# Layer 0's experts: which parts of a routed product are transposed on TensorE, and when its results are evicted

## The chip, the cores and the metric

The kernel runs on one core of a Trainium2 chip. The metric is device microseconds from the start to the end of one execution, lower is better. Three runs of the kernel before gave 1381.71, 1381.80 and 1383.36 us, median 1381.8. The engines are TensorE (PE, with its weight loads PEld), VectorE (DVE), ScalarE (ACT), GpSimd (POOL) and SyncE (SP, which here only issues DMAs).

## The reference

Four layers follow one another, each an attention over a context and a feed-forward block, on x of 4 batches x 256 tokens x 256 columns, in float32. The change lies in the feed-forward block of layer 0, 64 "arrows" of rank 16:

```python
def _L0_ffn_ref(x, A, B, W, bias):
    TOPK = 4
    vecs = jnp.einsum('arh,bsh->bsar', A, x)
    arrows = jnp.linalg.norm(vecs, axis=-1)
    _, idx = jax.lax.top_k(arrows, TOPK)
    routes = jax.nn.one_hot(idx, arrows.shape[-1], dtype=x.dtype).sum(-2) / TOPK
    v = jnp.einsum('bsa,bsar->bsr', routes, vecs)
    delta = jnp.einsum('bsa,ajr,bsr->bsj', routes, B, v)
    base = jnp.einsum('bsh,jh->bsj', x, W) + bias
    return base + delta
...
x = x + _L0_ffn_ref(_layernorm(x, axis=-1), L0_ffn_A, L0_ffn_B, L0_ffn_W, L0_ffn_bias)
```

For a token s, delta is a product over 64 x 16 = 1024 terms: route of arrow a times v of rank r, times B. The kernel needs these 1024 numbers u[a, r] with tokens in columns, as the stationary operand of eight matmuls of 128 rows each.

## The kernel before

All work of the four engines PE, ACT, DVE and POOL stands in an order written out by hand: inside `tc.manual_schedule` each of these engines executes its instructions in the order of the program text. SP is not among them. A DMA started through `nc.gpsimd` takes its place in POOL's order, one through `nc.scalar` in ACT's.

**Attention 0** (loops from line 1707): for each batch b and each of four groups of heads, two steps i = 2 hg + kp. A step does `scores` (PE, then ACT exponentials), `values` of the group before and, each second step, `quotient` (two stream transposes, a reciprocal and a product on DVE, additions on POOL). Between the steps `between(b, i)` (line 1613) places other work: in batches 0 to 2 the projections of the next batch, with a chain on DVE, ACT and PE (`sum`, `power`, `root`, `scaled`, `transposed`), and in batch 3 the first work of the experts. PSUM is a ring of six banks for nearly everything (tag "ring") and two banks "o".

**Experts of layer 0**: the class `Arrows` (line 1471) handles one of 8 chunks of 128 tokens (chunk n is batch n // 2, half n % 2):
- `vectors` (1479): eight matmuls of 512 columns, then squares (1493) and copies (1494) on ACT into the two halves of a tile `two`.
- `routes` (1496): on DVE the sum of squares, the four largest, the 64 routes (1509), the product of the vectors with them (1511) and v (1513); on POOL the product u of routes and v, 128 x 1024 (1514), into the second half of `two`.
- `turned` (1516): eight transposes on PE (1522) and two ACT copies (1525) into `uT`.
- `output` (1527): matmuls with ww (1531) and with wb (1535) into a bank "o", the bias added on DVE (1537), and x_sb updated on POOL (1538).

Its input rows are normalised: `Norm` (915) computes statistics on DVE and a POW on POOL (928), `tokens` (930) the normalised rows on DVE, and `layernorm_T` (939) transposes them on PE with an ACT copy. The kernel also has `layernorm_aside` (969), which does the same with two DVE stream transposes and 16 DMAs from SP, used in later layers; its scratch tile `y` has one buffer.

The loop at line 1749 runs the chunks after attention 0. Into it are mixed the **folds** of layer 1's weights (`folding`, 1003): eight steps, each with matmuls `pm` and `pn`, ACT work and a copy on DVE (1033). Each pair of steps needs one of four sets of raw weights, loaded by `load_raw` (987) in four DMAs of 512, 128, 128 and 512 KB into tiles with two buffers; the call stands in `folding` when nobody loaded the set earlier. At the end come the norm of layer 1's first rows (`a1_0`), its transposition, the squares of the context on ACT, and then layer 1's attention.

## Time and profile before

| what | value |
|---|---|
| median of 3 runs | 1381.8 us (1381.71 to 1383.36) |
| the profiled execution, its own time | 1380.97 us |
| its span, first to last instruction | 1379.2 us |
| mean granted TensorE clock | 0.999 |
| end of attention 0's last values on PE | 137.46 us |
| end of the last expert output on PE | 220.46 us |
| product u of line 1514 on POOL | 1.93 us, 8 times |
| copy of two transposes' banks, line 1525 on ACT | 0.59 us median, 16 times |
| raw weights of layer 1 on SP, first issues | 153.72 us (two sets), 181.05, 192.29 us |
| raw weights of layer 2 on POOL | 0.74 to 0.81 us for most issues |

Times in the profile are microseconds from the start of the span. A row of a timeline gives the start, the busy time, the engine, the line of the kernel, the operation, the tile written and the tiles read, the shape and how many; in brackets, how long the engine had stood idle and which instruction released it. In the chain a row gives start, length and what ran. A float32 matmul shows as two passes, a transpose as one.

### The profile page before, as it was taken

To read this page: it belongs to the slowest core of one execution; us is meant where nothing else is said; L and a number is where in the kernel's file an instruction comes from. 1 tells how busy PE (TensorE), PEld (TensorE's weight loads), DVE (VectorE), ACT (ScalarE), POOL (GpSimd) and SP (SyncE) were. 2 spreads that over 40 slices of the span, in tenths; PEclk is the share of its full clock that TensorE was granted. 3 is DMA by queue.
4 is the path that set the end of the run, shared out by engine and by line. 5 is a ranking of instruction groups with operands and counts; after the bars stand their busy time and mean duration, and the time that the engine had idled before them with its cause. 6 is when DMAs were issued, how large, how long until landed. Compare 5 with 4: busy or idle time off the path is not lost.

```text
span 1379.2 us, 20227 instructions
## 1 busy us (share of the span) xinstructions
PE 1369.2 (99%) x7221; PEld 903.1 (65%) x7221; DVE 897.2 (65%) x2052; ACT 572.6 (42%) x1134; POOL 699.4 (51%) x848
## 2 busy tenths in 40 slices
PE   9999999999999999999999999999999999999997
PEld 7665676566656667887565666666975665666666
DVE  6767863666666557655676756558656758566675
ACT  5766454433343332256434333333364334333331
POOL 5223333566565445352577655566325676444660
PEclk9999999999999999999999999999999999999999
DMA  5000220300000001361120000000432000000001
GB/s 171 15 3 2 77 78 17 89 19 8 16 5 19 0 13 43 83 218 48 47 54 15 17 0 16 0 1 16 124 119 69 7 12 4 1 8 1 0 1 34
DMA packets 77907, 50.79 MB, mean 37 GB/s; under 512 B 40628, under 2 KB 72645, under 8 KB 77799
## 3 DMA queue, kind: packets, MB, share of 16 engines
q1 hardware_dynamic: 72262, 36.13, 9.6%
q0 software_dynamic: 4176, 12.24, 3.1%
q8 instruction: 59, 0.97, 0.3%
q10 hardware_dynamic: 1360, 1.05, 0.2%
q14 instruction: 50, 0.40, 0.1%
HBM read 38.78 MB, written 6.95 MB: 33 GB/s over the span
## 4 chain that ended last, share of the span: by engine, by line
PE 97%; POOL 2%; DVE 1%; issue 0%; ACT 0%; POOLq 0%; DVEq 0%
PE ps L1948 23%; PE po L1956 23%; PE paq L1918 6%; PE pao L1918 5%; PE pbq L1918 4%; PE pbo L1918 4%; PE ps L1401 3%; PE po L1411 2%; PE pyf L1535 2%; PE paf L1485 2%; PE pgu L2496 2%; PE pm L1014 2%; PE psh L2317 2%; PE py L2042 2%; PE pn L1030 1%; PE pb L2901 1%
## 5 line engine op out<-in xcount | busy, mean ns | idle before, releaser
L1967 POOL TENSOR_TENSOR half<-pT 128x1024 f32<-128x1024 f32 x93 | 218.4, 2349 | 282.8 <-ACT pT L1951 228.0
L1948 PE MATMUL ps<-qT,cT 128*128 128x512 f32 x768 | 345.6, 593 | 0.0
L1956 PE MATMUL po<-pT,c_sb 128*128 128x512 f32 x768 | 345.3, 592 | 0.0
L1951 ACT ACTIVATE pT<-ps,mbias 128x512 f32<-128x512 f32 x384 | 263.8, 687 | 164.0 <-PE ps L1948 147.3
L1956 PEld LDWEIGHTS po<-pT,c_sb 128*128 128x128 f32 x768 | 145.8, 190 | 183.2 <-issue 183.2
L1948 PEld LDWEIGHTS ps<-qT,cT 128*128 128x128 f32 x768 | 138.9, 190 | 138.4 <-issue 136.1
L1960 ACT COPY oT<-po 128x512 f32<-128x512 f32 x96 | 56.2, 586 | 265.2 <-PE po L1956 265.2
L2003 POOL TENSOR_TENSOR oT<-oT,wide 128x512 f32<-128x512 f32 x84 | 106.8, 1291 | 0.0
L1928 DVE TENSOR_TENSOR qT<-qT,paq 128x128 f32<-128x128 f32 x90 | 25.2, 280 | 87.1 <-ACT qT L1927 87.1
L1405 ACT ACTIVATE pT<-ps 128x512 f32<-128x512 f32 x128 | 66.0, 602 | 21.6 <-PE ps L1401 21.4
L1975 DVE TENSOR_TENSOR half<-half 128x512 f32<-128x512 f32 x96 | 71.9, 749 | 2.7 <-POOL half L1965 2.5
L1977 DVE STREAM_TRANSPOSE turned<-half 128x512 f32<-128x512 f32 x96 | 68.3, 711 | 6.3
L1918 PE MATMUL paq<-xnT_a,m_sb 128*128 128x128 f32 x360 | 71.3, 280 | 0.0
L1928 DVE TENSOR_TENSOR w<-w,pao 128x128 f32<-128x128 f32 x21 | 6.0, 285 | 99.2 <-ACT w L1927 99.2
L1918 PE MATMUL paq<-xx,m_x 128*128 128x128 f32 x360 | 69.6, 275 | 0.0
L1918 PEld LDWEIGHTS paq<-xnT_a,m_sb 128*128 128x128 f32 x360 | 57.5, 192 | 18.2 <-issue 9.2
L1981 DVE TENSOR_REDUCE sums<-turned 128x16 f32<-128x512 f32 x96 | 65.9, 686 | 3.3
L1918 PE MATMUL pao<-n_x,ox 128*128 128x128 f32 x336 | 65.0, 275 | 0.0
L1927 ACT COPY qT<-paq 128x128 f32<-128x128 f32 x90 | 23.9, 265 | 94.2 <-PE paq L1918 93.2
L1931 DVE TENSOR_TENSOR qT<-qT,pbq 128x384 f32<-128x384 f32 x90 | 49.8, 554 | 9.4
L1918 PEld LDWEIGHTS paq<-xx,m_x 128*128 128x128 f32 x360 | 54.7, 192 | 0.0
L2002 DVE STREAM_TRANSPOSE wide<-rz 128x512 f32<-128x512 f32 x84 | 54.4, 686 | 0.0
(504 smaller groups left out, 2553.9 us busy)
## 6 DMA issues: line engine op xcount, KB each, us to landing
wq<-in_L_wqT SPq DMA_DIRECT2D x8, 512.0 KB
wo<-in_L_wo SPq DMA_DIRECT2D x8, 512.0 KB
yd<-yr SPq DMA_DIRECT2D x20, 128.0 KB
xnT_a<-y_a SPq DMA_DIRECT2D x144, 16.0 KB
xd<-xn_f SPq DMA_DIRECT2D x8, 256.0 KB
w<-in_F_w SPq DMA_DIRECT2D x4, 512.0 KB
wq<-in_L_wqT POOLq DMA_DIRECT2D x3, 512.0 KB
wo<-in_L_wo POOLq DMA_DIRECT2D x3, 512.0 KB
```

Of the source, the lines that this page charges most:

```text
L1405: nc.scalar.activation(pT[kp][:, j], ps[j], AF.Exp)
L1918: nc.tensor.matmul(p[:, at, :], lhsT=lhsT, rhs=rhs, start=(k == 0 and at == 0), stop=(k == len(of) - 1 and i == which[-1]),)
L1948: nc.tensor.matmul(ps, lhsT=cT[:, b, k * P : (k + 1) * P], rhs=qT, start=True, stop=True)
L1951: nc.scalar.activation(pT[:, k, :], ps, AF.Exp, bias=mbias[:, b, k : k + 1])
L1956: nc.tensor.matmul(po, lhsT=c_sb[:, b, k, :], rhs=pT[:, k], start=(k == 0), stop=(k == NK - 1))
L1960: done["head"] = nc.scalar.copy(raw, po).ins
L1967: nc.gpsimd.tensor_tensor(half, pT[:, 0:2], pT[:, 2:4], ALU.add)
L1975: nc.vector.tensor_tensor(part, half[:, 0], half[:, 1], ALU.add)
L1977: nc.vector.transpose(turned.rearrange("p f i -> p (f i)"), part)
L1981: nc.vector.tensor_reduce(sums[b, hp // 4][:, hp % 4, :], turned, AX.X, ALU.add)
L2002: nc.vector.transpose(wide, rzs[b, hp // 4][:, hp % 4, :, None].to_broadcast([P, NB, 32]))
L2003: eng.tensor_tensor(outs[b, hp], outs[b, hp], wide.rearrange("p f i -> p (f i)"), ALU.mult)
```

## The change

- `routes` no longer forms u. It leaves the routes twice side by side (128 columns) and v (16 columns). `turned` transposes only these two on PE; v's transpose goes by an ACT copy and a DMA to a DRAM tile `turned_v`, and SP reads it back so that each of 128 partitions (64 arrows, two halves) holds 8 ranks by 128 tokens in the second half of `two`. A new `spread` multiplies this in place by the transposed routes on POOL, which gives uT. wb is loaded with its rows permuted to match.
- `output` is split: the matmuls stay, the bias and the addition to x_sb become `add`, called later.
- The expert rows of batches 0 to 2 go by `layernorm_aside` (new `rows_of_arrows`), the first already in batch 2 of attention 0. Chunk 0's `vectors` move from step 4 of batch 3 to step 1, its `routes` from 5 to 2, and its `turned` and `spread` come before the end of attention 0.
- The loop over chunks is replaced by a sequence written out. Raw weights of layer 1 are loaded by POOL instead of SP, one set at a time, behind the spreads of chunks 2, 3, 4 and 6.

```diff
-            dma = (nc.gpsimd if L == 2 else nc.sync).dma_start(dst, src[a * P : (a + z) * P, :].rearrange("(h e) d -> e h d", e=P))
+            dma = (nc.gpsimd if L < 3 else nc.sync).dma_start(dst, src[a * P : (a + z) * P, :].rearrange("(h e) d -> e h d", e=P))
...
+        dram0 = ctx.enter_context(tc.tile_pool(name="f0d", bufs=1, space=bass.MemoryType.DRAM))
...
-        wb = load_fw("wb", [P, 8, D], lambda w: [(w, t["F0_bT"].rearrange("(k p) n -> p k n", p=P))], "wb", f0w)
+        wb = load_fw("wb", [P, 8, D], lambda w: [
+            (w[64 * h : 64 * h + 64], t["F0_bT"].rearrange("(a h k) n -> h a k n", h=2, k=8)[h]) for h in range(2)
+        ], "wb", f0w)
...
+        turned_v = dram0.tile([B * NC, RA, P], F32, tag="turned_v", name="turned_v")
...
-                route = small.tile([P, NA], F32, tag="route", name=f"route{u}")
-                nc.vector.tensor_scalar(route, rest[:, :NA], 0.0, 1.0 / TOPA, ALU.is_lt, ALU.mult)
-                route_b = route[:, :, None].to_broadcast([P, NA, RA])
-                nc.vector.tensor_tensor(ar, ar, route_b, ALU.mult)
-                v = small.tile([P, RA], F32, tag="v", name=f"v{u}")
-                nc.vector.tensor_reduce(v, ar.rearrange("p a r -> p r a"), AX.X, ALU.add)
-                nc.gpsimd.tensor_tensor(sq, route_b, v[:, None, :].to_broadcast([P, NA, RA]), ALU.mult)
+                self.route = sq.rearrange("p a r -> p (a r)")[:, : 2 * NA].rearrange("p (h a) -> p h a", h=2)
+                nc.vector.tensor_scalar(
+                    self.route, rest[:, None, :NA].to_broadcast([P, 2, NA]), 0.0, 1.0 / TOPA, ALU.is_lt, ALU.mult
+                )
+                nc.vector.tensor_tensor(ar, ar, self.route[:, 0, :, None].to_broadcast([P, NA, RA]), ALU.mult)
+                self.v = small.tile([P, RA], F32, tag="v", name=f"v{u}")
+                nc.vector.tensor_reduce(self.v, ar.rearrange("p a r -> p r a"), AX.X, ALU.add)
 
             def turned(self):
-                self.uT = w0.tile([P, 8, P], F32, tag="qT0", name=f"uT{self.u}")
-                for n in range(2):
-                    pt = bank("t", [P, 4, P], f"puT{self.u}_{n}")
-                    for k in range(4):
-                        a0 = 8 * (4 * n + k)
-                        nc.tensor.transpose(
-                            pt[:, k, :], self.two[:, 1, a0 : a0 + 8, :].rearrange("p a r -> p (a r)"), ident
-                        )
-                    nc.scalar.copy(self.uT[:, 4 * n : 4 * n + 4, :], pt)
+                two = self.two.rearrange("p n a r -> p n (a r)")
+                self.routeT, vT = two[:, 0, :P], two[:RA, 0, P : 2 * P]
+                self.uT = two[:, 1].rearrange("p (k s) -> p k s", s=P)
+                pt = bank("t", [P, 2, P], f"prT{self.u}")
+                nc.tensor.transpose(pt[:RA, 1, :], self.v, ident)
+                nc.tensor.transpose(pt[:, 0, :], self.route.rearrange("p h a -> p (h a)"), ident)
+                nc.scalar.copy(vT, pt[:RA, 1, :])
+                put = turned_v[self.b * NC + self.c]
+                nc.scalar.dma_start(put, vT)
+                nc.scalar.copy(self.routeT, pt[:, 0, :])
+                for h in range(2):
+                    nc.sync.dma_start(
+                        two[64 * h : 64 * h + 64, 1],
+                        put[8 * h : 8 * h + 8].rearrange("(o k) s -> o (k s)", o=1).to_broadcast([64, 8 * P]),
+                    )
+
+            def spread(self):
+                nc.gpsimd.tensor_tensor(
+                    self.uT, self.uT, self.routeT[:, None, :].to_broadcast([P, 8, P]), ALU.mult
+                )
...
+        def rows_of_arrows(k):
+            xnT = early.tile([P, ND, S], F32, tag="xf", name=f"xnT_f0_{k}", bufs=3)
+            xnTs["f", k] = layernorm_aside(norms["f"].tokens(), f"f0_{k}", xnT, True)
...
+            if b == B - 2:
+                if i == 2:
+                    norms["f"] = Norm(0, "f0_0")
+                elif i == 3:
+                    rows_of_arrows(0)
...
-                if i in (0, 2, 6):
-                    norms["f", i // 2] = Norm(min(i // 2, 2), f"f0_{min(i // 2, 2)}")
-                if i in (1, 3, 7):
-                    xns["f", i // 2] = norms["f", i // 2].tokens()
-                if i in (3, 5):
-                    k = (i - 3) // 2
-                    xnTs["f", k] = layernorm_T(xns["f", k], f"f0_{k}")
-                if i == 4:
+                if i in (0, 6):
+                    norms["f"] = Norm(1 + i // 6, f"f0_{1 + i // 6}")
+                if i in (1, 7):
+                    rows_of_arrows(1 + i // 6)
+                if i == 1:
                     arrows[0] = Arrows(0)
                     arrows[0].vectors()
+                if i == 2:
+                    arrows[0].routes()
                 if i == 5:
-                    arrows[0].routes()
+                    arrows[0].turned()
+                if i == 7:
+                    arrows[0].spread()
...
         for n in (1, 2):
             arrows[n] = Arrows(n)
             arrows[n].vectors()
-        arrows[1].routes()
-        arrows[0].turned()
+            arrows[n].routes()
         arrows[0].output()
+        arrows[1].turned()
+        arrows[0].add()
         output0(B - 1)
...
+        def vectors(n):
+            arrows[n] = Arrows(n)
+            arrows[n].vectors()
+
+        def output(n, *raw):
+            arrows[n].spread()
+            for i in raw:
+                load_raw(1, i)
+            arrows[n].output()
...
+        vectors(3)
+        norm = Norm(3, "f0_3")
+        arrows[2].turned()
+        vectors(4)
+        vectors(5)
+        arrows[3].routes()
+        arrows[4].routes()
+        output(1)
+        arrows[3].turned()
+        output(2, 0)
+        arrows[1].add()
+        xn3 = norm.tokens()
+        arrows[5].routes()
+        arrows[4].turned()
+        arrows[2].add()
+        next(fold)
+        xnTs["f", 3] = layernorm_T(xn3, "f0_3")
+        next(fold)
+        vectors(6)
+        output(3, 1)
+        arrows[5].turned()
+        arrows[6].routes()
+        arrows[3].add()
+        vectors(7)
+        context_squares(0)
+        arrows[7].routes()
+        output(4, 2)
+        arrows[6].turned()
+        context_squares(1)
+        arrows[4].add()
+        next(fold)
+        next(fold)
+        norm = Norm(0, "a1_0")
+        arrows[7].turned()
+        xn1 = norm.tokens()
+        output(5)
+        context_squares(2)
+        arrows[5].add()
+        output(6, 3)
+        context_squares(3)
+        arrows[6].add()
+        for _ in range(3):
+            next(fold)
+        first_xnT = layernorm_T(xn1, "a1_0")
+        next(fold)
+        output(7)
+        arrows[7].add()
         next(fold, None)
```

More of the change, by code (lines that the diff above doesn't have):

```diff
@@ L1535, in output, with add @@
                     nc.tensor.matmul(py, lhsT=self.uT[:, k, :], rhs=wb[:, k, :], start=False, stop=(k == 7))
+                self.py = py
+            def add(self):
+                b, c, py = self.b, self.c, self.py
                 ys = w0.tile([P, D], F32, tag="y_sb", name=f"ys{self.u}")
@@ L1747, in bounded_path @@
         fold = folding(1, *mn)
-        for n in range(B * NC):
-            if n + 2 < B * NC:
-                arrows[n + 2].routes()
-            if n:
-                arrows[n].turned()
-            if n % NC == 0:
-                if n + 3 < B * NC:
-                    arrows[n + 3] = Arrows(n + 3)
-                    arrows[n + 3].vectors()
-                for _ in range((0, 0, 1, 1, 2, 2, 1, 1)[n]):
-                    next(fold)
-                if n == 6:
-                    xn1 = norm.tokens()
-                if n:
-                    arrows[n].output()
-            else:
-                k = n // NC + 2
-                if k < B:
-                    xnTs["f", k] = layernorm_T(xns["f", k + (k == 2)], f"f0_{k}")
-                if n == 7:
-                    first_xnT = layernorm_T(xn1, "a1_0")
-                    next(fold)
-                arrows[n].output()
-                for _ in range((0, 0, 1, 1, 2, 2, 1, 0)[n]):
-                    next(fold)
-                if n + 3 < B * NC:
-                    arrows[n + 3] = Arrows(n + 3)
-                    arrows[n + 3].vectors()
-            if n == 5:
-                norm = Norm(0, "a1_0")
-            if n == 0:
-                norm = Norm(3, "f0_3")
-            if n == 1:
-                xns["f", 3] = norm.tokens()
-            if 2 <= n < 2 + B:
-                b = n - 2
-                c2 = w0.tile([P, NK, DC], F32, tag="z0", name=f"c2_{b}")
-                for k in range(NK):
-                    nc.scalar.activation(
-                        c2[:, k], c_sb[:, b, k], AF.Square, accum_out=csq[:, b * NK + k : b * NK + k + 1]
-                    )
@@ new lines, in vectors, with context_squares @@
+        def vectors(n):
[6 more added lines that the diff above has]
+            arrows[n].output()
+        def context_squares(b):
+            c2 = w0.tile([P, NK, DC], F32, tag="z0", name=f"c2_{b}")
+            for k in range(NK):
+                nc.scalar.activation(
+                    c2[:, k], c_sb[:, b, k], AF.Square, accum_out=csq[:, b * NK + k : b * NK + k + 1]
+                )
```

## The prediction

> **What bounds the kernel.** First I read the busy times and the chain that ended last:
> ```profile
> PE 1369.2 (99%) x7221; PEld 903.1 (65%) x7221; DVE 897.2 (65%) x2052; ACT 572.6 (42%) x1134; POOL 699.4 (51%) x848
> ...
> PE 97%; POOL 2%; DVE 1%; issue 0%; ACT 0%; POOLq 0%; DVEq 0%
> ```
> TensorE is the chain. Then the busy time of the stretch that changes, from the end of attention 0 to the last expert output:
> ```profile
> 137.46:220.46 83.00, 83.00 (x381) 60.79 (x382) 57.99 (x109) 41.08 (x119) 26.02 (x24) 1.00 0.21 64
> ```
> The columns are PE, PEld, DVE, ACT, POOL, clock, DMA. PE is busy in all 83.00 us: a matmul removed shortens the kernel by its own length, and a wait added to PE lengthens it by its own. Third, the chain in order of time (start, us, what):
> ```profile
> 113.97 0.16 PE pmk L1680
> ...
> 116.10 1.75 PE ps L1401 x16
> ...
> 119.88 1.07 PE ps L1401 x16
> ...
> 144.52 0.87 PE puTf L1522 x8
> ...
> 155.93 0.44 PE pxn_f L945 x4
> ```
> Fourth, DVE and POOL in order of time, whose order is that of the program:
> ```profile
> 206.18 0.69 DVE L1033 COPY n_sb<-pn 128x512 f32<-128x512 f32 x1 [1.06 <-PE pn L1030]
> 206.78 0.42 DVE L925 BATCH_NORM_STATS2 st_a<-x_sb 128x6 f32<-128x256 f32 x1
> ...
> 208.23 0.70 POOL L928 TENSOR_TENSOR rstd_a<-ve_a,neghalf 128x2 f32<-128x2 f32 x1 [2.13 <-DVE ve_a L927]
> ...
> 213.12 0.42 DVE L1537 TENSOR_TENSOR ysf<-pyf,bias 128x256 f32<-128x256 f32 x1 [2.98 <-PE pyf L1535]
> 213.62 0.73 POOL L1538 TENSOR_TENSOR x_sb<-x_sb,ysf 128x256 f32<-128x256 f32 x1 [4.69 <-DVE ysf L1537]
> ```
> Here a fold's copy, a norm and its POW on POOL, then an addition on POOL hold nobody up, since no matmul needs POOL soon after. In the new program one does.

> **Removed from TensorE.** Eight transposes of an arrow take 0.87 us (0.109 each); two remain, 0.22. Over 8 arrows: 8 x 0.65 = 5.2 us. Three `layernorm_T` for the expert rows go to DVE and DMAs: in the chain they took 0.59, 0.44, 0.44 = 1.47 us. The 1.75 us of scores after `pmk` against 1.07 elsewhere was a wait for DVE to empty the mask's bank; `vectors` of arrow 0 now stands between (3.43 us) and covers it: 0.68. **Gain: 7.35 us.** All other matmuls stay: `vectors` 3.43, `output` 0.86 + 3.45 = 4.31, a fold 0.89 + 0.86.

> **The new way of uT.** Two transposes, an ACT copy (0.25), a DMA issue on ACT (0.5 at the start of the trace), 8 KB to DRAM, two reads of 256 KB issued by SP (0.5 each), then `spread` on POOL. No row times a DMA to DRAM and back. The only load with a waiting reader is x_sb, 256 KB: issued at 0.80, first used at 3.92, so 3.1 us. Two such in sequence and the issues give about 7.1 us; below, two rows of issue alone, 1.5; above, a raw set of 1.3 MB needed 5.9 us from issue to the end of its traffic, so 12.5. I take 7.1, the nearest by size. `spread` has no row: the old product of the same size took 1.93 (two repeated operands), the addition of line 1967, also 128x1024, 2.35. With contiguous operands it is nearer to the second, and the additions of 256 and 512 columns (0.73, 1.27) extrapolate there too: 2.35, low end 1.93.

> Let T be the end of attention 0's last values (137.46 before). By the rows, PE's order after T is: vectors 1, 2; output 0; turned 1 (T+11.4); output0; vectors 3; turned 2 (16.8); vectors 4, 5; output 1 (23.7 to 28.0); turned 3; output 2 (28.2 to 32.5); turned 4; fold, transposes, fold; vectors 6 (ends 40.1); output 3. Each `output` starts with 0.86 us of ww matmuls that need no uT. Outputs 1, 2 and 3 then need `spread` finished at T+24.6, 29.1 and 41.0. Reads land at T+18.5, 23.9 and 35.3; POOL is free of the additions and the POW of batch 3's norm at T+19.6; of arrow 2's addition, behind five `routes` of 5.4 us on DVE, at T+37.5. So those spreads end at about T+22, 26.3 and 39.9: hidden, by 2.6, 2.8 and 1.1. If that cover goes, each late us is one on PE. Outputs 0 and 7 have over 4 us.

> **The waits added.** Three spreads stand on POOL behind something that only just became possible.
> Output 4: `spread` follows arrow 3's addition, which follows `routes` 6 on DVE. From the end of vectors 6: routes start after 0.67 and take 5.43 (row 185.98 to 191.43), ysf 0.42, x_sb 0.81, spread 2.40: 9.7. PE gets there after 4.31 + 0.22 + 3.43 + 0.86 = 8.8. **Wait 0.9** (0.45 with 1.93).
> Output 5: behind it on POOL is the POW of layer 1's norm; its statistics wait on DVE for the copy of the second fold just before. From the end of `pn`: copy to POW 206.14 to 208.93, 2.79, plus 2.40 = 5.2; PE has 0.22 + 0.86. **Wait 4.1** (3.7).
> Output 6: `spread` follows arrow 5's addition. From the end of output 5 the rows give 213.08 to 214.35, 1.27, plus 2.40 = 3.67, less 0.86. **Wait 2.8** (2.4).
> Sum 7.8 (6.5 to 7.8). Behind spread 5 POOL has arrow 5's addition, spread 6 and raw set 3, all of which only follow output 5 anyway; DVE's `tokens` behind the POW feed a transpose much later.

> **Smaller terms.** In batch 2, tokens (1.14 beside a POOL addition) and two stream transposes (0.83) now stand on DVE ahead of the head sums; the chain sum, power, root, pad ends at 102.85 instead of 101.9, PE wants it at 102.38, and the late exponentials hold banks: 0.5 (0 to 1.2). In batch 3, `routes` 0 on DVE delays two evictions by about 0.5 and 0.4 past the reuse of their banks: 0.6 (0 to 0.9). Raw set 0 is issued by POOL (0.75 to 0.81 a piece, 3.1 in all) only after spread 2, from T+26.3; SP's last piece landed 4.4 after its issue, so wo at T+33, just when `pn` wants it (33.6), beside the reads of arrow 3 (512 KB): 0.5 (0 to 2.5). The later sets have 5 us or more from the wait of their buffers, and SP's own queue carries 16 pieces of expert rows (0.65 each) ahead of arrow 1's reads: done at T+12.8, no later than the write. The last rows land near T+15, needed at T+16.8. The permuted wb load and 4 MB of reads ride on a DMA share of 0.21: nothing. ACT loses 1.1 us of copies an arrow and gets two short ones and an issue: nothing.

> **Sum.** 7.8 + 0.5 + 0.6 + 0.5 = 9.4 of waits against 7.35 gained: +2.05 us (-0.85 to +5.05). The profiled execution took 1380.97 (span 1379.2 and 1.8 around it), 0.8 under the median 1381.8; a difference carries over, so **1383.8**. 0.2%, 2.8 us, is about what a measurement of this kernel can tell from no change; the forecast lies within that.

> **Rivals.** (A) The forecast, 52%: the gain is real and POOL's order gives it back; own range 1380.9 to 1386.9.
> (B) Slower: the pause before output 5 lets the matrix clock fall. This trace has a slow TensorE once, after the idle start:
> ```profile
> 1.53 4.21 PE L1468 MATMUL pwarm<-ident 128*128 128x128 f32 x18 [1.53 <-POOL ident masks.py:199]
> ...
> 7.96 0.83 PE L1468 MATMUL pwarm<-ident 128*128 128x128 f32 x6
> ```
> 0.23 us a pass, later 0.11, for some 6 us, so half of 6 is lost: 3.0, giving 1386.8. It decides if 4.1 us of idle is enough; in the stretch no gap is over 0.3 us and the clock column reads 1.00, so nothing there speaks for or against. 16%.
> [...]
> (C) Slower: the DRAM round trip takes 12.5 instead of 7.1. It decides from 9.9 (29.1 - 2.4 - 16.8), where output 2's slack ends; then output 1 waits 1.7 (11.4 + 12.5 + 2.4 against 24.6), output 2, now later, 0.9, and the first fold, its weights issued behind, 2.2 in place of 0.5: +4.3, 1388.1. For it: SP and raw sets share the queues; against: the DMA share. 8%.
> (D) Faster: the three waits don't arise, because DVE or POOL comes earlier than the rows say. The gain less the smaller terms is 5.75: 1376.0. Against it: in this trace POOL and DVE keep the program's order everywhere in the stretch. That the change doesn't take work off PE can't be: the transposes are gone from its program. 24%.

> **Chances.** Of A's 52%, 0.45 lies beyond +2.8, 0.53 within and 0.02 below -2.8; B and C are slower, D faster: slower 0.47, same 0.28, faster 0.25. The range reaches down to 1375, 1 below D's value, and up to 1389, 0.9 above C's; what is left out is a bound met together with a rival.

> **What would show it.** Right: PE idle ahead of uT's matmuls three times, released by POOL's spread, near 1, 4 and 3 us; two transposes per arrow; the stretch from T to the last output near 85.5 (83.0, less 5.4 of transposes and 0.44, plus 8.3 of waits); matmuls of 0.109 a pass after the pauses. Wrong: no idle before outputs 5 and 6 (D); passes of 0.2 us behind output 5's pause (B); idle before outputs 1 to 3 released by a DMA (C); spread at another price than 1.93 to 2.35.

## The result, and the profile after

| | before | after |
|---|---|---|
| median | 1381.8 us, 7 runs, 1380.28 to 1383.45 | 1386.19 us, 7 runs, 1385.75 to 1387.07 |
| profiled execution, its span | 1380.97, 1379.2 us | 1386.06, 1384.3 us |
| mean granted TensorE clock of the profiled execution | 0.999 | 0.994 |

The changed kernel takes 1.0033 of the time before, 95% interval 1.0023 to 1.0044: some 4.4 us longer. The forecast was 1383.8 us, range 1375 to 1389.

The page of after, the busy times and the chain, against the same two lines of before:

```profile
PE 1368.5 (99%) x7161; PEld 900.0 (65%) x7161; DVE 900.4 (65%) x2058; ACT 567.1 (41%) x1131; POOL 714.0 (52%) x864
...
PE 95%; POOL 2%; DVE 1%; issue 1%; ACT 0%; POOLq 0%; DVEq 0%
```

PE has 60 rows less and is busy 0.7 us less, in a span 5.1 us longer. The stretch from the end of attention 0's last values to the last expert output (start and end, length, then PE, PEld, DVE, ACT, POOL busy, clock, DMA share, GB/s):

```profile
136.45:224.36 87.91, 80.22 (x329) 56.11 (x328) 56.42 (x103) 35.88 (x116) 40.48 (x39) 0.96 0.37 106
```

Before, PE was busy in all of its 83.00 us. Now 7.7 of 87.91 are idle, and the clock column, 1.00 before, reads 0.96. The rows of PE in order of time show both (start, busy time, what, and in brackets the idle time ahead and what ended it):

```profile
186.45 3.72 PE L1551 MATMUL pyf<-wb,twof 128*128 128x256 f32 x16 [0.86 <-POOL twof L1539]
...
199.06 6.21 PE L1551 MATMUL pyf<-wb,twof 128*128 128x256 f32 x16 [4.08 <-POOL twof L1539]
205.11 1.03 PE L1547 MATMUL pyf<-ww,xnT_f 128*128 128x256 f32 x4
208.88 3.72 PE L1551 MATMUL pyf<-wb,twof 128*128 128x256 f32 x16 [2.75 <-POOL twof L1539]
```

The brackets are the three waits for `spread`, ahead of outputs 4, 5 and 6. The second row takes 6.21 us where its neighbours take 3.72 for the same 16 passes: from 199.06 to the next row's 205.11 are 6.05 us, against 3.45 at full clock without a pause, so 2.60 lost (its neighbours, which start after a pause at full clock, lose 0.11 of that too). The clock in windows of 1 us (the last three columns are clock, DMA share, GB/s):

```profile
197.00:198.00 1.00, 0.00 (x0) 0.00 (x0) 1.00 (x1) 1.00 (x9) 1.00 (x1) 0.65 0.06 11
198.00:199.00 1.00, 0.00 (x0) 0.00 (x0) 1.00 (x1) 0.47 (x4) 1.00 (x1) 0.50 0.00 0
...
204.00:205.00 1.00, 1.00 (x6) 0.90 (x5) 0.00 (x0) 0.00 (x0) 0.00 (x0) 0.93 0.00 0
205.00:206.00 1.00, 1.00 (x6) 0.65 (x4) 0.42 (x1) 0.00 (x0) 0.19 (x1) 1.00 0.00 0
```

It falls to a half at 197.31, while PE is idle, and is back at 204.13.

A second low passage lies 375 us later, in layer 1, where the lists of tokens per expert are made. Before, and then after, PE in order of time:

```profile
565.47 4.07 PE L2429 MATMUL plist<-bring,at 128*128 128x40 f32 x32
569.37 2.84 PE L2335 MATMUL pysh<-wds,gsT 128*128 128x256 f32 x12
```

```profile
569.42 4.61 PE L2482 MATMUL plist<-bring,at 128*128 128x40 f32 x32
573.82 5.47 PE L2388 MATMUL pysh<-wds,gsT 128*128 128x256 f32 x12
```

Nothing waits here in either kernel, and the change doesn't touch these lines. Yet the twelve wide passes take 5.26 us to the next row instead of 2.68, and the whole place costs 3.3 us more, of which 0.3 comes back in the expert blocks behind it.

A third difference lies at the very start, ahead of everything that the change touches. The first matmuls run slowly in both (the first 18 passes take 4.21 us), and full speed comes sooner in the profiled execution of after. Before, and then after:

```profile
6.38 1.30 PE L1468 MATMUL pwarm<-ident 128*128 128x128 f32 x6
```

```profile
6.28 0.83 PE L1471 MATMUL pwarm<-ident 128*128 128x128 f32 x6
```

After is 0.4 us ahead from here on, by chance: in another execution of a kernel made from before, raw weights on POOL below, arrow 0's vectors start at 122.36, in before at 122.85.

So the 5.1 us of span add up from places where the same instruction can be compared in both traces: -1.0 at the end of attention 0 (first vectors at 137.39 and 136.39; -0.4 of it from the start), +4.9 in the stage (first matmul of layer 1 at 220.30 and 224.20, so +3.9), +3.0 at the lists and behind, together +6.95 at the last matmul (1371.32 and 1378.27); then -1.85, since the end of the program comes 7.2 us after the last matmul in before and 5.3 in after.

### The profile page after: what moved, and what is told of

The parts are those of the page before. It is cut to its first block, busy times and chain, and to the rows that moved or that the text cites. A ratio compares the mean times of both kernels' runs of the same rounds, so it can differ in the third digit from the quotient of the medians.

```text
span 1384.3 us, 20261 instructions
## 1 busy us (share of the span) xinstructions
PE 1368.5 (99%) x7161; PEld 900.0 (65%) x7161; DVE 900.4 (65%) x2058; ACT 567.1 (41%) x1131; POOL 714.0 (52%) x864
## 4 chain that ended last, share of the span: by engine, by line
PE 95%; POOL 2%; DVE 1%; issue 1%; ACT 0%; POOLq 0%; DVEq 0%
PE ps L2001 23%; PE po L2009 23%; PE paq L1971 6%; PE pao L1971 5%; PE pbq L1971 4%; PE pbo L1971 4%; PE ps L1404 3%; PE po L1414 2%; PE paf L1490 2%; PE pgu L2549 2%; PE psh L2370 2%; PE pyf L1551 2%; PE py L2095 2%; PE pm L1014 1%; PE pn L1030 1%; PE pb L2954 1%
## 5 line engine op out<-in xcount | busy, mean ns | idle before, releaser
L928 POOL TENSOR_TENSOR rstd_f<-ve_f,neghalf 128x2 f32<-128x2 f32 x15 | 10.6, 705 | 85.6 <-DVE ve_f L927 84.7
```

## The experiments

Each kernel was run beside the kernel before on the same chip; ratios are to before, with 95% intervals. "At the lists" is the start of the first `plist` matmul, 565.47 in before and 569.42 in after: what a trace shows there is what layer 0 gained or lost, give or take some 0.4 us by which executions of the same work differ from the start on (arrow 0's vectors start at 113.96 to 114.40 in after and the kernels made from it).

**The pause before output 5.** Layer 1's first norm is moved behind output 5.

```diff
-        norm = Norm(0, "a1_0")
         arrows[7].turned()
-        xn1 = norm.tokens()
         output(5)
+        norm = Norm(0, "a1_0")
+        xn1 = norm.tokens()
```

> Layer 1's first Norm and its tokens are put behind output(5), so output 5's spread is issued on POOL before the Norm's power and rstd work. Theory 1 (the stage lost its time to the pause of 4.08 us before output 5's wb matmuls, and to the clock of 0.50 that followed it, 2.6 us more): the pause is under 1 us and the clock stays at 1.00, so the stage is about 6 us shorter than after's 87.8; 1386.2 - 4.1 - 2.6 = 1379.5, or about 1376.5 if the second low clock (572.7 to 578.8 in after) goes too. Rival (the pause is only the place where lateness shows, and layer 1's first attention waits for its Norm instead): the pause goes, but tokens come some 4 us later and PE waits for them: 1383 to 1386.

Measured: 1379.78 us (0.9987, 0.9979 to 0.9996). The pause before output 5 is gone, and nobody waits for the norm. PE of this kernel:

```profile
195.22 3.62 PE L1551 MATMUL pyf<-wb,twof 128*128 128x256 f32 x16
...
202.45 5.41 PE L1551 MATMUL pyf<-wb,twof 128*128 128x256 f32 x16 [2.75 <-POOL twof L1539]
```

The total is as theory 1 had it, its parts aren't: the same pause of 2.75 us before output 6 that left the clock alone in after halves it here, for half as long (1.7 us lost). So the length of a pause alone does not decide.

**The pause kept, but filled.** Dummy matmuls stand between output 5's ww and wb matmuls.

```diff
-            def output(self):
+            def output(self, fill=0):
...
+                if fill:
+                    warm(fill)
...
-            arrows[n].output()
+            arrows[n].output(17 if n == 5 else 0)
```

> Seventeen transposes' worth of empty matmuls of 128x128 stand between output 5's ww and wb matmuls; all else is after's. Theory 1 (the low clock is made by PE's idle time before output 5): wb's matmuls start as late as in after, but run at 1.00, 3.4 to 3.7 us instead of 6.05; 1386.2 - 2.6 = 1383.6, or 1380.5 if the second low clock goes as well. Rival (the low clock is not tied to the idle time, but to a time in the program): wb's matmuls take 6 us all the same, and the time is 1386 or more.

Measured: 1384.75 us (1.0025, 1.0015 to 1.0036), 1.1 above the expectation. PE:

```profile
195.39 3.96 PE L1471 MATMUL pwarm<-ident 128*128 128x128 f32 x34
199.65 3.72 PE L1553 MATMUL pyf<-wb,twof 128*128 128x256 f32 x16 [0.30 <-POOL twof L1539]
203.20 1.03 PE L1547 MATMUL pyf<-ww,xnT_f 128*128 128x256 f32 x4
206.98 5.41 PE L1553 MATMUL pyf<-wb,twof 128*128 128x256 f32 x16 [2.75 <-POOL twof L1539]
```

Output 5's matmuls start as late as in after but at full clock, 3.72 us against 6.21: the low clock there comes from the idle time. What is missing to the expectation is output 6's: its pause of 2.75 us now lowers the clock, which costs 1.7 us (the lists, with one low stretch instead of two, give some of it back).

**All spreads ahead of what made them late.**

```diff
+        arrows[4].spread()
+        load_raw(1, 2)
         arrows[6].routes()
...
-        output(4, 2)
+        arrows[4].output()
...
-        norm = Norm(0, "a1_0")
         arrows[7].turned()
-        xn1 = norm.tokens()
         output(5)
+        arrows[6].spread()
+        load_raw(1, 3)
+        norm = Norm(0, "a1_0")
+        xn1 = norm.tokens()
...
-        output(6, 3)
+        arrows[6].output()
```

> All three late spreads are issued on POOL ahead of what made them late: output 4's before routes 6 and add 3, output 6's and 5's before layer 1's Norm. Theory 1 (the three waits of 0.86, 4.08 and 2.75 us and the low clock of 2.6 us are the whole loss of the change; turning only routes and vectors gains about what was forecast): 1386.2 - 7.7 - 2.6 = 1375.9, and 1372.7 if the second low clock goes too: faster than before by 6 to 9 us. Rival (the waits cover others, for the Norm's tokens or for raw weights, that end just behind them): under 4 us of it is gained, 1382 or more.

Measured: 1374.79 us (0.9949, 0.9936 to 0.9962), 7.0 us below before. At the lists it stands at 561.57, 3.9 us ahead of before and 7.85 ahead of after. Its trace has no low clock between the start and the last matmul. Two waits are left, 1.79 us before output 5 and 0.24 before output 6:

```profile
196.22 3.72 PE L1551 MATMUL pyf<-wb,twof 128*128 128x256 f32 x16 [1.79 <-POOL twof L1539]
...
201.04 3.72 PE L1551 MATMUL pyf<-wb,twof 128*128 128x256 f32 x16 [0.24 <-POOL twof L1539]
```

POOL shows a new cause:

```profile
193.82 2.35 POOL L1539 TENSOR_TENSOR twof<-twof 128x1024 f32<-128x1024 f32 x1 [0.65 <-DMA twof<-turned_v]
198.63 2.36 POOL L1539 TENSOR_TENSOR twof<-twof 128x1024 f32<-128x1024 f32 x1 [2.47 <-DMA twof<-turned_v]
```

POOL is there in time and waits for the vectors to come back from DRAM. For output 5 that took 12.2 us from the last transpose (181.59) to the spread. In after, arrow 2's trip, the only one with a wait of POOL for it, took 7.3 (153.16 to 160.48). Raw set 2 is loaded at the same time here, and the reads of `turned_v` take up to 7.2 us from issue to landing, against at most 4.0 in after.

**The spread in halves.**

```diff
-                nc.gpsimd.tensor_tensor(
-                    self.uT, self.uT, self.routeT[:, None, :].to_broadcast([P, 8, P]), ALU.mult
-                )
+                for k in (0, 4):
+                    nc.gpsimd.tensor_tensor(
+                        self.uT[:, k : k + 4], self.uT[:, k : k + 4],
+                        self.routeT[:, None, :].to_broadcast([P, 4, P]), ALU.mult,
+                    )
```

> Each spread is done as two instructions of four blocks, so that wb's first four matmuls can start after the first half. Theory 1: each of the three pauses ends about 1.2 us sooner (0, 2.9 and 1.6 us), the second half (1.2 us) ends before the first four pairs of matmuls (1.7 us) do; if the clock goes low after 4.08 us and not after 2.75, it may stay up at 2.9: 1386.2 - 3.3 - 2.6 = 1380.3, and 1382.9 if it still goes low. Rival (PE waits for the whole tile whichever half is done, or the second instruction's own start costs what the half saves): 1386, within 0.5 us.

Measured: 1382.11 us (1.0003, 0.9995 to 1.0012), runs from 1379.2 to 1383.7. The waits are 0, 3.00 and 1.68 us, each 0.9 to 1.1 shorter, so PE does start on the first half.

```profile
196.82 5.12 PE L1553 MATMUL pyf<-wb,twof 128*128 128x256 f32 x16 [3.00 <-POOL twof L1540]
```

The clock falls after 3.00 us, for one time of 3.4 us instead of two. The profiled run, the fastest of the twelve, has no low clock at the lists.

**What lowers the clock at the lists.** The next two kernels are before and after with six filling matmuls, which stand ahead of the list matmuls, split into three ahead and four in the middle.

```diff
-                for _ in range(6):
+                for _ in range(3):
                     nc.tensor.matmul(pw, lhsT=ident, rhs=ident, start=True, stop=True)
                 for n in units:
+                    if n == 8:
+                        for _ in range(4):
+                            nc.tensor.matmul(pw, lhsT=ident, rhs=ident, start=True, stop=True)
```

> The kernel before, with its six filling matmuls ahead of layer 1's list matmuls (128x40, 3.9 us without a wide one among them) split: three ahead, four in the middle (0.2 us more PE work). Theory 1 (the clock is set for one stretch of 3.41 us by how busy PE's array was in the stretch ahead of it; the list matmuls fill one such stretch in some runs and not in others, and each low stretch costs 1.7 us: that is why before's runs stand at about 1380.4, 1382.0 and 1383.6): no run has a low stretch, all lie at 1380.3 to 1381.0, clock 0.998 to 0.999. Rival (the low stretch comes from something else, power or the chip's state): the runs still spread over 1380 to 1384.

> After, with the same split of the filling matmuls; all in layer 0 stays. Theory 1: the second low clock (572.8 to 579.6, 2 stretches, 3.2 us) goes and the first (197.3 to 204.1) stays: 1386.2 - 3.2 + 0.2 = 1383.2, clock 0.997, one low passage in the trace. Rival (the second low clock follows from the first, or from anything in layer 1 but the list matmuls): 1386, two low passages.

Measured: before so mixed 1381.19 us (0.9992, 0.9983 to 1.0), after so mixed 1383.56 (1.0017, 1.0008 to 1.0025). Of the 72 runs of before beside the experiments (a 73rd, at 2841.94 us, is left out) 29 stand at 1380.2 to 1381.0, 29 at 1381.5 to 1382.5 and 14 at 1383.3 to 1384.0. Of the 11 mixed ones ten stand in one group at 1380.8 to 1381.6, up to 0.6 above the range expected, and one at 1382.8; that one was profiled, has no low clock, and lost 1.4 us in the expert blocks at 593 us, where the mix does nothing. After comes down by 2.6 us. PE of after so mixed:

```profile
569.20 2.11 PE L2485 MATMUL plist<-bring,at 128*128 128x40 f32 x16 [0.24 <-DVE at L2484]
571.14 1.14 PE L2479 MATMUL pfill<-ident 128*128 128x128 f32 x8
572.11 1.88 PE L2485 MATMUL plist<-bring,at 128*128 128x40 f32 x16
573.82 2.84 PE L2388 MATMUL pysh<-wds,gsT 128*128 128x256 f32 x12
```

The wide passes behind the lists are back at 2.84. Theory 1 holds for both: with wide matmuls among the narrow ones the twelve passes behind take 2.84 us, without them 5.47 in after, though PE is busy there all the time.

**The raw set moved out of the trip's way** (on the kernel with the spreads first).

```diff
         arrows[4].spread()
-        load_raw(1, 2)
...
-        output(5)
+        output(5, 2)
```

> The kernel with the spreads first, but raw set 2 of layer 1 is loaded behind output 5's spread instead of output 4's, so that it no longer fills the DMA queues while output 5's vectors go through DRAM. Theory 1 (that trip took 11.6 us instead of 7.2 because the raw loads moved at the same time, 1.79 us of PE's wait): the trip is 7 to 8 us, PE's wait before output 5 goes, 1374.8 - 1.8 = 1373.0. Rival (output 6's trip collides with the load instead, or the fold waits for the raw set): 1374.5 to 1377, the wait stands before output 6 or in the fold.

Measured: 1375.8 us (0.9959, 0.9946 to 0.9973). Theory 1 is right about the trip, and the rival about the time. The traffic of output 5's vectors, 512 KB, lies alone between 185.5 and 188.5, so that the trip from the last transpose (181.28) takes about 7 us (columns as in the windows above):

```profile
185.50:188.50 3.00, 3.00 (x16) 2.64 (x15) 2.73 (x10) 1.76 (x10) 0.73 (x1) 1.00 0.62 175
188.50:192.00 3.50, 3.50 (x24) 2.85 (x23) 3.46 (x4) 2.06 (x11) 0.35 (x1) 1.00 0.01 2
```

The spreads of outputs 5 and 6 don't wait for DRAM any more, but PE still waits 0.64 us before output 5 (POOL does arrow 4's addition first), 0.68 before output 6 (its spread stands behind the 2.95 us in which POOL issues set 2), and 0.5 in a fold (for an addition on DVE). Layer 1 begins at 216.38, as without the edit (216.36), though arrow 0's vectors start 0.3 sooner here.

**The removed transposes put back** (on the kernel with the spreads first).

```diff
+                pw = bank("mm", [P, P], "pwarm")
+                for _ in range(6):
+                    nc.tensor.transpose(pw, ident, ident)
                 nc.scalar.copy(vT, pt[:RA, 1, :])
```

> The kernel with the spreads first, with six transposes of 128x128 more in every turn, of the identity into a bank that nobody reads: the work that the change took off PE is put back. Theory 1 (these transposes stood on PE's path, so their removal is worth 8 x 0.65 = 5.2 us, less what PE's 2.0 us of waits swallow): 1374.8 + 3.9 to 5.2 = 1378.7 to 1380.0. Rival (PE had room for them, the gain comes from the order): under 2 us, 1375 to 1376.8.

Measured: 1378.46 us (0.9976, 0.9966 to 0.9985), 3.7 above the first runs of the kernel without them, 2.1 above its second set of runs below; the three sets were run on three chips. Two of the ten runs, at 1381, have low clock in them. In the traces output 5 begins so, without the transposes and then with them:

```profile
193.40 1.03 PE L1547 MATMUL pyf<-ww,xnT_f 128*128 128x256 f32 x4
```

```profile
198.13 1.03 PE L1550 MATMUL pyf<-ww,xnT_f 128*128 128x256 f32 x4
```

4.73 of the 5.2 us stand on PE's path. Behind it the two waits end, 2.0 us, and layer 1 begins 2.2 us later (218.53 and 216.36).

**Spreads first and in halves; and the raw weights alone.** The first joins the two edits shown above. The second is before with one line of the change:

```diff
-            dma = (nc.gpsimd if L == 2 else nc.sync).dma_start(...)
+            dma = (nc.gpsimd if L < 3 else nc.sync).dma_start(...)
```

> The kernel with the spreads first, with each spread in two halves besides. Theory 1 (PE's two waits there, 1.79 and 0.24 us, end with the first half, 1.2 us sooner): 0.6 us of wait is left, 1374.8 - 1.4 = 1373.4. Rival (what waits less there waits for the fold of the raw weights behind, or the eight more instructions on POOL give the gain back): 1374.3 to 1375.5.

> The kernel before, with layer 1's raw weights issued by POOL instead of SP, at before's places: that part of the change alone. On POOL a set takes 2.95 us to issue (0.79 + 0.70 + 0.71 + 0.75), and a set waits for its buffer, with the products of the routes and vectors behind it. Theory 1 (the part alone is a loss at before's places, and pays only with the loads put where POOL has time): products late by 3 to 6 us, 1383 to 1388. Rival (POOL, busy 26 of the stage's 83 us, has room for it): within 1 us of before. The end of the run: last matmul to the end takes 7.2 us in before and 5.3 in after; if raw weights on SP's queue make this difference, it is 5.4 here, else 7.2.

> The kernel with the spreads first once more, beside the one with halves. Theory 1 (its first five runs, 1373.9 to 1375.1, stand for it): median 1374.3 to 1375.2. Rival (five runs happened to be without a low stretch of the clock at the list matmuls; before had one or two in 14 to 21 of its runs): some runs at 1376.5 and 1378, median up to 1376.5.

Measured: with halves 1375.98 us (0.9963, 0.995 to 0.9975), without them 1376.32 (0.9957, 0.9943 to 0.9971). At the lists the halves gain 1.35 us against the first trace without them (560.22 and 561.57), of which 0.3 is there from the start (arrow 0's vectors at 114.03 and 114.35); the second trace without them stands at 562.50. The runs hide the gain: three of six stand at 1377.0 to 1377.6, three of the five without halves at 1376.3 to 1377.7, and the profiled one of these shows the low clock at the lists. The rival on luck was right: the first five runs had been spared. The second trace also has a wait that the first hasn't, for raw set 0:

```profile
171.50 1.10 PE L1030 MATMUL pn<-wo,wv 128*128 128x512 f32 x2 [0.86 <-DMA wo<-in_L_wo]
```

Raw weights on POOL alone: 1430.52 us (1.0354, 1.034 to 1.0369), over 40 us above what either theory gave. The waits of PE in its stage, and POOL at the first load:

```profile
PE pm L1014 <- DMA wk<-in_L_wkT: 37.1, 4, 13.1
```

```profile
174.39 1.92 POOL L1514 TENSOR_TENSOR twof<-routef,vf 128x1024 f32<-128x1024 f32 x1 [5.62 <-DVE vf L1513]
176.26 0.85 POOL L998 DMA_DIRECT2D wq<-in_L_wqT  x1
```

On SP the first set was issued at 153.72. On POOL it stands behind the products, each of which waits for DVE; the fold asks for it at 168 and gets it at 181. In the changed kernel the loads stand behind the spreads, and in its trace PE doesn't wait for them. The long waits also hold the clock down, to 0.984 in the mean. The last matmul lies 6.9 us before the end here, so SP's queue doesn't explain the shorter end of after.

**A version without the low clock.** Spreads first and in halves, and a product of shared expert 1 moved from behind the list matmuls to between them.

```diff
+                    if n == 10:
+                        shared[1].down(0)
...
-            shared[1].down(0)
```

> The kernel with the spreads first and in halves, and in layer 1 the six matmuls of shared expert 1's first down product (1.3 us, wide) stand between the tenth and eleventh list matmul pair instead of behind the last; no work is added. Theory 1 (one stretch of 3.41 us without wide matmuls is what lowers the clock there): no run has a low stretch at the lists, all runs at 1373.5 to 1375.2, clock 0.999 or more; of the kernels with the spreads first, 6 of 16 runs stood at 1376.3 to 1377.7. Rival (the lists end 1.3 us later and the gathers of the experts' rows come late by it): 1375 to 1376.5 in all runs.

Measured: 1374.69 us (0.9957, 0.9944 to 0.9971), five runs at 1374.2 to 1375.7. Both sides are seen. No run stands at 1376.3 or above, and the trace has no low clock between the start and the last matmul (five runs are few: 10 of the 16 without this edit stood below 1376.3 too); but a gather comes late:

```profile
580.34 0.41 PE L2532 MATMUL pxg<-ident,xg 128*128 128x128 f32 x2 [0.48 <-DMA xg<-xd,who]
```

It is 5.7 us faster than before in its own comparison, and its median lies 11.5 below after's.

## Why the prediction was right, and where it was not

*Transposes, 5.2 us.* Right: put back, 4.73 of them show on PE, and 2.2 behind the waits that they cover.

*Three waits on POOL, 0.9, 4.1 and 2.8.* Right to a tenth: 0.86, 4.08, 2.75, behind the instructions named. With the spreads ahead of these, layer 0 gains 7.85 us, where the waits and the low clock had cost 10.3; 2.0 come back as new waits, and 0.3 is that trace's later start.

*Spread 2.35, trip 7.1 us.* Spreads took 2.33 to 2.40, the trip 7.3 where POOL waited for it; outputs 1 to 3 wait for nothing in after. The upper bound of 12.5 is no idle fear: it came to 12.2 beside a raw set.

*Smaller terms, 1.6.* Too high. In batch 2 a group of scores takes 1.80 instead of 1.15 us (0.65, forecast 0.5), but the next but one takes 1.44 instead of 1.77. In batch 3 the group that took 1.82 takes 1.41: 0.4 gained, where the forecast had 0.68 for the mask's bank less 0.6 for delayed banks. Raw set 0 (0.5) costs nothing in after, and 0.86 in one trace of the kernel with the spreads first.

*The stretch, forecast 85.5.* 87.91 less 2.60 of low clock is 85.3. At full clock the change would have lost 1.3 us by layer 1 (3.9 - 2.6), and without the chance of the start 1.7, against 2.05 forecast. That is the forecast's own mechanism.

*Rival B, 16%, 3.0 us.* It came true on top of A: 2.60 us. The step that failed is that A and B were set against each other, and B's condition was put as "if 4.1 us of idle is enough". The forecast of 1383.8 is by this 2.6 too low.

*The lists, +3.0.* Not foreseen. The prediction read the clock in the stretch that changes and held the rest for constant. It isn't: before's runs stand at three heights, with a mean clock of 0.998 to 0.999 at the lowest and 0.996 at the highest, and at one height, but for one run, with the lists mixed. Its profiled execution, on which the sum was built, is one without a low passage at the lists.

*The end, -1.85.* Not foreseen either, and its cause is open: 6.9 to 7.2 us from the last matmul to the end in before and the two kernels made from it, 5.2 to 5.5 in after and those made from it.

By these terms: 1380.97 - 0.4 (the start) + 1.7 + 2.6 + 3.0 - 1.85 = 1386.0, measured in the profiled run 1386.06. The median of 1386.19 lies in the range of 1375 to 1389, a wide one, and 2.4 above the forecast. That it comes so near is in part luck: low clock, which the forecast left out, adds 5.6 us, and an end and a start that were not foreseen either take 2.25 back.

## What to carry to other kernels

An operation moved to another engine has that engine's whole queue ahead of it (here that made waits of 0.86, 4.08 and 2.75 us): write down what stands in front of it there, and put it ahead of whatever waits for something later. Here a few lines moved turn a loss of 4.4 us into a gain of 7 (5.0 in a second set of runs). And before a difference of 2 or 3 us is laid to a change, look at the granted clock over the whole span in both traces, the first microseconds included.

## What the hardware showed that was not expected

**Low clock came in stretches of 3.41 us.** The low passages lasted 3.41 us (norm behind output 5: 203.81 to 207.22; spread in halves: 196.27 to 199.68), twice that (after: 197.31 to 204.13) and up to four times that (raw weights on POOL: 172.86 to 186.52). In three traces with two low passages, these begin 375.47 us apart (after: 197.31, 572.77), 365.23 (norm behind: 203.81, 569.03) and 365.23 (pause filled: 208.16, 573.38): 110.0, 107.0 and 107.0 times 3.4133, half of after's low passage. At a clock of 0.50 each lost half of the time that PE worked in it, up to 1.7 us a stretch (5.41 us for a row that takes 3.72 at full clock). The passages begin elsewhere in each of these traces. From their starts, PE's share of idle time in the stretch ahead can be worked out from the rows:

| kernel, stretch | idle in it | clock in the next |
|---|---|---|
| after, 193.89 to 197.31 | 2.33 us, 68% | half |
| after, 197.31 to 200.72 (at half clock) | 1.76, 52% | half |
| after, 204.13 to 207.54 | 1.41, 41% | full |
| norm behind, 200.40 to 203.81 | 2.06, 60% | half |
| pause filled, 204.74 to 208.16 | 2.24, 66% | half |
| spread in halves, 192.85 to 196.27 | 2.45, 72% | half |
| after, lists mixed, 194.14 to 197.56 | 1.75, 51% | full |
| after, lists mixed, 197.56 to 200.97 | 2.34, 69% | half |

**A small trip through DRAM depends on its neighbours.** 8 KB out and 512 KB back took 7.3 us, and 12.2 with 1.3 MB of weights loading beside; with that load moved away the reads were done after about 7 again. The raw sets and the reads were not in one queue, as rival C had it: in after, from 160 to 172 us, set 0 is in q0 (1.31 MB) and arrow 3's reads in q1 (0.52 MB).

Open: why all seven runs of after stand at a mean clock of 0.994 to 0.995, like the profiled one with its low passage at the lists, when a part of the runs of before and of the reordered kernels has none there; and the 1.8 us at the end of the program.
